# Layer 0's node loop: loads queued behind the x tiles, degree sums on TensorE, reciprocal by Ln and Exp

## The chip, the cores and the metric

The kernel runs on one core of a Trainium2 chip. The metric is the device time of one execution in microseconds; the time of a kernel is the median of several runs. Profiles come from one profiled execution each. TensorE is written PE, VectorE DVE, ScalarE ACT, GpSimd POOL and SyncE SP, as in the profile.

## What is computed

The reference is a network of four layers, each `x = x + layer(relu(layernorm(x)))`, over x of 8 batches × 2048 nodes × 64 features with a 0/1 adjacency of 2048 × 2048. Only layer 0, attention over the hyperedges of an incidence matrix H (2048 × 64), is touched:

```python
h = x @ W                                   # x: layernorm and relu done
alpha = softmax(where(H.T > 0, leaky_relu(h @ a_node), NEG))   # over nodes
agg = einsum('ben,bnf->bef', alpha, h)
beta = sigmoid((h @ a_gn)[:, None, :] + (agg @ a_ge)[:, :, None])
all_he = elu(beta[..., None] * h[:, None] + (1 - beta[..., None]) * agg[:, :, None])
deg = maximum(adj.sum(-1), 1.0)[:, None]
industry = einsum('nm,bmf->bnf', adj / deg, x @ W_ind)
coefs1 = softmax(where(H > 0, attn_scores(elu(agg)), NEG))
g = einsum('bne,benf->bnf', coefs1, all_he)
coefs2 = softmax(attn_scores(stack([industry, g])))
out = einsum("bnk,bnkf->bnf", coefs2, stack([industry, g]))
```

Layers 1 (graph attention), 2 (three message steps) and 3 (node-wise weights) follow and use the same adjacency.

## The kernel before

**Tiling.** P is 128 partitions, and the 2048 nodes are NT = 16 tiles of 128. A node tile of x has all 8 batches beside each other, 128 × 512. The 8 batches × 64 features are also NP = 4 blocks of 128 in the transposed form hn[p]. The adjacency is read in NCW = 4 chunks of CW = 512 columns, each as eight pairs of row tiles `at` (512 KB a load, through POOL's DMA queue, six buffers, `rows_of` at L893). `acc[p]` are the four PSUM sums of one chunk.

**Layer 0's loop** (L976 to L990) norms the 16 x tiles, maps them by W_ind and at once multiplies them into chunk 0 of the adjacency. It is software-pipelined over 21 iterations j, and each step has a lag in tiles: `sums` (DVE reduce and scale), `centred` (POOL subtraction, xc), `squares` (ACT), `sums2` (DVE reduce), `scales` (ACT Ln, Exp), `scaled` (DVE, xc times the scale), `turns` (PE, four transposes into tpx), `turned` (ACT, four copies into hn), `maps` (PE, four matmuls into py), `halves` (ACT copy to Y[0], DVE rest to Y[1]), and `spread` (PE, eight matmuls into acc). `degrees` (L963) adds the adjacency pairs on POOL into ds. x tiles are loaded through SP by `load`, three tiles ahead, five buffers. M (H, two loads) and MT (H transposed, `HT`) are loaded through SP ahead of the loop, at L972 to L974.

**Order.** Inside the loop the steps are issued through `InOrder` wrappers V, A and G (L622), which keep program order on DVE, ACT and POOL; with `kit.strict` PE's matmuls keep it too. Instructions issued otherwise are placed by a scheduler, which may move them ahead in their engine's queue, as far as their data and buffers allow. In the kernel before, SP's loads are of this second kind, and so are `weights` (L810, the small weights of the layer), `marks` (L1172, `is_gt 0` on M and MT), `listing` (hyperedge ranks) and what follows.

**Behind the loop** `out_of(0)` (L1023) empties chunk 0, and `industry(c)` (L1004) does chunks 1 to 3, 128 matmuls each. Between its matmuls it takes small jobs off a list `units`, three for each adjacency pair: for each node tile `members` (the W matmuls ph, split in hi and lo parts, which go to hi_dram and lo_dram through SP, and sums for agg), the listing, the weights of layers 1 and 2 with their loads, and hyperedge tables. `out_of` copies acc to ev, sums ds over partitions by two matmuls with ones (deg), takes twice the maximum with 1 (rdeg), its reciprocal on DVE, multiplies the four ev by it and stores them to ind_dram. Then the phase over node tiles and slots begins with `nodes(0)` (ACT tmp, POOL sT), `ranks` (PE px), `edges` (DVE oT) and the pm matmuls, and copies xT to x1_dram in DRAM for layer 1.

Of the kernel before, what the change touches and what calls it, by code (L numbers as in the profile page):

```python
# [16 lines left out]
P = 128  # L17
B, N, F = 8, 2048, 64
E = 64
NP = B // 2  # L20
# [614 lines left out]
class Kit:  # L635


    def __init__(self, tc, t, pool):
        nc = self.nc = tc.nc
        self.tc, self.t, self.strict = tc, t, False  # L640
# [24 lines left out]
    def column(self, pool, src, name):  # L665
        c = pool.tile([P, 1], FP, name=name)
        for b2 in range(2):
            self.nc.sync.dma_start(out=c[half(b2), :], in_=src)
        return c
# [5 lines left out]
    def block_diag_in(self, w, src):  # L675
        self.nc.vector.memset(w, 0.0)
        for b2 in range(2):
            self.nc.sync.dma_start(out=w[half(b2), half(b2)], in_=src)
        return w

    def layer1_weights(self, pool, ps):

        nc, t = self.nc, self.t
# [3 lines left out]
        nc.vector.memset(a4, 0.0)  # L687
        for b2 in range(2):
            nc.sync.dma_start(out=a4[half(b2), b2 : b2 + 1], in_=t["L1_gnn_a"][F : 2 * F, :])
            nc.sync.dma_start(out=a4[half(b2), 2 + b2 : 3 + b2], in_=t["L1_gnn_a"][0:F, :])  # L690
# [5 lines left out]
    def layer2_weights(self, pool, ps):  # L696

        nc, t, mm = self.nc, self.t, self.nc.tensor.matmul
# [3 lines left out]
        W2n = self.block_diag(pool, t["L2_gnn_W2"], "W2n", "wd")  # L702
        for dst, src in ((self.b1, "b1"), (self.b2c, "b2"), (self.ivc, "intervention_value")):
            for b2 in range(2):
                nc.sync.dma_start(out=dst[half(b2), :], in_=t[f"L2_gnn_{src}"])

        for dst, w in ((self.Wvc, self.W1v), (self.Wec, self.W1e)):
# [51 lines left out]
def layer0(kit, hn, x1_dram, open_early, late_tile, between):  # L759
# [9 lines left out]
    w0 = ctx.enter_context(tc.tile_pool(name="v0", bufs=1, reuse_waits="tile"))  # L769
    dram = ctx.enter_context(tc.tile_pool(name="h_dram", bufs=1, space=DRAM))  # L770
# [29 lines left out]
    with ExitStack() as sA:  # L800
# [9 lines left out]
        def weights(pool, ps):  # L810

            W = kit.block_diag(pool, t["L0_gnn_W"], "W0f", "wd")
            WT = kit.block_diag(pool, t["L0_gnn_WT"], "W0Tf", "wt")
            a2 = pool.tile([P, 4], FP, name="a2")
            nc.vector.memset(a2, 0.0)
            for b2 in range(2):
                nc.sync.dma_start(out=a2[half(b2), b2 : b2 + 1], in_=t["L0_gnn_a_node"])
                nc.sync.dma_start(out=a2[half(b2), 2 + b2 : 3 + b2], in_=t["L0_gnn_a_gn"])
            nc.sync.dma_start(out=a_ge, in_=t["L0_gnn_a_ge"].rearrange("f o -> o f").to_broadcast([P, F]))
            nc.sync.dma_start(out=fcb, in_=t["L0_gnn_fcb"])  # L820
            nc.sync.dma_start(out=av, in_=t["L0_gnn_av"])
            for b2 in range(2):
                nc.sync.dma_start(out=fcW[half(b2), :], in_=t["L0_gnn_fcW"])
            nc.vector.tensor_scalar(Av, ones, av, None, op0=OP.mult)
            nc.vector.tensor_copy(Wx[:, 0:P], W)
            pw = ps.tile([P, 4], FP, tag="ph", name="pw", bufs=2)
            mm(pw, WT, a2, start=True, stop=True)
            nc.vector.tensor_copy(Wx[:, P : P + 4], pw)

        def listing(ps):  # L830
# [4 lines left out]
            def slots():  # L835
                tmp = lst.tile([P, SLOTS], mybir.dt.int32, tag="hhi", name="iota_i", bufs=3)
                nc.gpsimd.iota(tmp, pattern=[[1, SLOTS]], base=0, channel_multiplier=0)
                nc.vector.tensor_copy(slot, tmp)
# [3 lines left out]
                nc.vector.tensor_copy(tri, ti)  # L842
# [47 lines left out]
        aps = sA.enter_context(tc.tile_pool(name="a_ps", bufs=1, space=PSUM, reuse_waits="tile"))  # L890
        accs = lambda: [aps.tile([P, CW], FP, tag=f"acc{p}", name=f"acc{p}") for p in range(NP)]
# [9 lines left out]
        with ExitStack() as s1:  # L901
            sb = s1.enter_context(tc.tile_pool(name="nf_sb", bufs=2, reuse_waits="tile"))
            ps = s1.enter_context(tc.tile_pool(name="nf_ps", bufs=2, space=PSUM, reuse_waits="tile"))
            V, A, G = InOrder(tc, nc.vector), InOrder(tc, nc.scalar), InOrder(tc, nc.gpsimd)
            acc, ds = accs(), dsp.tile([P, 2, CW], FR, tag="ds", name="ds")
# [4 lines left out]
            def load(i):  # L910
                xs[i] = sb.tile([P, B * F], FP, tag="x", name="x", bufs=5)
                nc.sync.dma_start(out=xs[i], in_=t["xN"][i * P : (i + 1) * P, :])
# [25 lines left out]
            def turns(i):  # L938
                tp[i] = ps.tile([P, NP, P], FP, tag="tp", name="tpx")
# [22 lines left out]

            def degrees(g):  # L963
                if g:
                    G.tensor_tensor(ds, (at[0] if g == 1 else ds).bitcast(FP), at[g].bitcast(FP), op=OP.add)
# [6 lines left out]
            for h in range(2):  # L972
                nc.sync.dma_start(out=M[:, :, h, :], in_=t["L0_gnn_H"].rearrange("(t p) e -> p t e", p=P))
            nc.sync.dma_start(out=MT, in_=t["HT"])  # L974
            kit.strict = True
            for j in range(NT + 5):  # L976
                on = lambda k: 0 <= j - k < NT
                if 0 < j and j + 3 < NT:
                    load(j + 3)
                for lag, step in (  # L980
                    (0, sums), (0, centred), (1, squares), (1, sums2), (2, turns), (3, maps),
                    (4, halves), (1, scales), (1, scaled), (2, turned), (5, spread),
# [4 lines left out]
                if m > 0 and m % 2:  # L987
                    degrees(m // 2)
                    if 1 <= m // 2 and m // 2 + 5 < NT // 2:
                        at[m // 2 + 5] = rows_of(0, m // 2 + 5)  # L990
            kit.strict = False

        with ExitStack() as s1:
            sb = s1.enter_context(tc.tile_pool(name="e_sb", bufs=2, reuse_waits="tile"))
            ps = s1.enter_context(tc.tile_pool(name="e_ps", bufs=1, space=PSUM, reuse_waits="tile"))
            ones_r = sb.tile([P, P], FR, name="ones_r", bufs=1)
            for h in range(2):
                nc.vector.tensor_copy(ones_r[:, half(h)], ones)
# [5 lines left out]
            def industry(c):  # L1004

# [1184 lines left out]
```

## Time and profile before

| | us |
|---|---|
| median of 3 runs (lowest, highest) | 2018.38 (2016.62, 2019.0) |
| profiled execution, its time | 2020.19 |
| profiled execution, its span | 2018.3 |
| PE busy in the span | 1926.3 (95%) |
| DVE, ACT, POOL busy | 1232.7 (61%), 437.2 (22%), 343.2 (17%) |
| chunk 0's loop: first and last acc matmul | 40.1, 95.5 |
| end of chunk 3's acc matmuls | 257.0 |

The span is what the profiler saw of the program; 1.9 us of the execution lie around it. Busy times of engines overlap. Row L630 and row L723 are lines of helpers that issue on behalf of many steps, so groups are told apart by the names of their tiles. "A<-B" reads: written A, read B.

### The profile page before, as it was taken

To read this page: it belongs to the slowest core of one execution; us is meant where nothing else is said; L and a number is where in the kernel's file an instruction comes from. 1 tells how busy PE (TensorE), PEld (TensorE's weight loads), DVE (VectorE), ACT (ScalarE), POOL (GpSimd) and SP (SyncE) were. 2 spreads that over 40 slices of the span, in tenths; PEclk is the share of its full clock that TensorE was granted. 3 is DMA by queue.
4 is the path that set the end of the run, shared out by engine and by line. 5 is a ranking of instruction groups with operands and counts; after the bars stand their busy time and mean duration, and the time that the engine had idled before them with its cause. 6 is when DMAs were issued, how large, how long until landed. Compare 5 with 4: busy or idle time off the path is not lost.

```text
span 2018.3 us, 23591 instructions
## 1 busy us (share of the span) xinstructions
PE 1926.3 (95%) x9092; PEld 1148.0 (57%) x9092; DVE 1232.7 (61%) x1940; ACT 437.2 (22%) x907; POOL 343.2 (17%) x446
## 2 busy tenths in 40 slices
PE   3899999987999999999999999999999999999997
PEld 3777767632322222226776467775477755577653
DVE  5867489966899999893234752326632356523365
ACT  3422145557211111111130011210111200112100
POOL 3511057621000000000001210002200012101022
PEclk9999889999999999999999999999999999999999
DMA  7467256156212222214110012201022100122000
GB/s 185 147 183 206 85 174 200 47 151 146 67 48 58 48 58 53 53 43 102 53 48 18 22 38 65 58 13 31 23 64 61 32 21 20 44 68 57 4 20 12
DMA packets 85786, 142.41 MB, mean 71 GB/s; under 512 B 33232, under 2 KB 33488, under 8 KB 82992
## 3 DMA queue, kind: packets, MB, share of 16 engines
q1 hardware_dynamic: 65200, 83.86, 14.3%
q0 software_dynamic: 20464, 56.96, 11.3%
q8 instruction: 73, 1.20, 0.2%
q14 instruction: 49, 0.40, 0.1%
HBM read 106.84 MB, written 37.09 MB: 71 GB/s over the span
## 4 chain that ended last, share of the span: by engine, by line
PE 59%; issue 20%; DVE 8%; DMA 7%; ACT 3%; POOL 2%; SPq 1%; POOLq 0%; DVEq 0%; ACTq 0%
PE acc L723 23%; PE u L723 13%; PE o L723 3%; PE pd L723 3%; PE pgs L723 2%; PE acc L1013 2%; PE py L723 2%; DMA den<-d_dram 2%; DMA at<-in_adjT 2%; PE dn L723 1%; PE pm L723 1%; DVE xc L630 1%; PE mean L723 1%; PE var L723 1%; DVE pt L1663 1%
## 5 line engine op out<-in xcount | busy, mean ns | idle before, releaser
L723 PE MATMUL acc<-aT,parts 128*128 128x512 f32 x1664 | 448.3, 415 | 0.0
L723 PEld LDWEIGHTS acc<-aT,parts 128*128 128x128 f32 x1664 | 306.5, 188 | 102.2 <-issue 39.8
L2065 DVE TENSOR_TENSOR pr<-u,embf 128x512 f32<-128x512 f32 x256 | 170.6, 687 | 170.8 <-PE u L723 163.8
L1663 DVE SCALAR_TENSOR_TENSOR pt<-R,wd,aT 128x1024 f32<-128x1024 f32 x192 | 235.9, 1277 | 9.5 <-DMA R<-r_dram 2.7
L723 PE MATMUL u<-W3f,y 64*128 64x512 f32 x1024 | 241.2, 589 | 0.0
L723 PE MATMUL o<-pt,hS 128*64 128x512 f32 x1024 | 237.3, 599 | 0.8 <-DVE pt L1663 0.6
L723 PEld LDWEIGHTS u<-W3f,y 64*128 64x128 f32 x1024 | 99.8, 187 | 120.0 <-issue 120.0
L723 PEld LDWEIGHTS o<-pt,hS 128*64 128x64 f32 x1024 | 68.3, 136 | 160.1 <-issue 148.6
L723 PE MATMUL u<-W3f,v 64*128 64x512 f32 x512 | 135.8, 607 | 0.0
L2077 POOL TENSOR_TENSOR fold<-fold 128x256 f32<-128x256 f32 x64 | 47.7, 746 | 505.8 <-DVE fold L2076 505.8
L723 PE MATMUL dn<-pt,vd 128*32 128x512 f32 x1024 | 123.1, 598 | 0.0
L1882 DVE TENSOR_TENSOR yb<-py,cb_f 128x512 f32<-128x512 f32 x32 | 22.1, 691 | 161.3 <-PE py L723 161.3
L1013 PE MATMUL acc<-at,Y 128*128 128x512 f32 x384 | 109.1, 425 | 1.1 <-DVE ev L1026 1.1
L723 PE MATMUL acc<-aTl,parts 128*128 128x512 f32 x384 | 96.5, 393 | 0.0
L1972 POOL TENSOR_TENSOR bq<-bq,xp 128x512 f32<-128x512 f32 x16 | 20.6, 1287 | 433.5 <-ACT xp L1955 433.5
L2069 DVE TENSOR_TENSOR pr<-pr 128x512 f32<-128x512 f32 x128 | 88.1, 688 | 2.2
L1663 DVE SCALAR_TENSOR_TENSOR pt<-R,wd,aTl 128x1024 f32<-128x1024 f32 x64 | 79.8, 1281 | 12.4 <-PE dn L723 8.2
L723 PEld LDWEIGHTS u<-W3f,v 64*128 64x128 f32 x512 | 50.5, 186 | 55.9 <-issue 34.1
L1013 PEld LDWEIGHTS acc<-at,Y 128*128 128x128 f32 x384 | 71.6, 196 | 18.2 <-issue 3.5
L723 PEld LDWEIGHTS acc<-aTl,parts 128*128 128x128 f32 x384 | 72.1, 188 | 16.9
L630 POOL TENSOR_TENSOR mix<-ex,wt 128x512 f32<-128x512 f32 x64 | 67.8, 1061 | 34.6 <-DVE ex L630 27.6
L723 PEld LDWEIGHTS dn<-pt,vd 128*32 128x32 f32 x1024 | 26.9, 108 | 80.9 <-issue 76.3
(343 smaller groups left out, 2758.5 us busy)
## 6 DMA issues: line engine op xcount, KB each, us to landing
at<-in_adjT POOLq DMA_DIRECT2D x32, 512.0 KB, 5.1
raw<-in_adjT SPq DMA_DIRECT2D x64, 256.0 KB, 3.4
aT<-in_adjT POOLq DMA_DIRECT2D x12, 1024.0 KB, 5.2
xp<-xd SPq DMA_DIRECT2D x45, 256.0 KB, 3.4
R<-r_dram SPq DMA_DIRECT2D x14, 512.0 KB, 3.7
hi_dram<-hi SPq DMA_DIRECT2D x16, 264.0 KB, 3.0
lo_dram<-lo SPq DMA_DIRECT2D x16, 264.0 KB, 3.3
hlo<-lo_dram POOLq DMA_DIRECT2D x16, 264.0 KB, 3.2
```

The lines of the kernel that those rows point to most:

```text
L630: self.tc.keep_in_program_order(getattr(self.engine, name)(*args, **kw))
L723: one = self.nc.tensor.matmul(*args, **kw)
L1013: mm(acc[p], Y[h][:, m, p, :], at[:, k, :], start=m + h == 0, stop=m == NT - 1 and h == 1)
L1663: nc.vector.scalar_tensor_tensor(pt, R[b2], wd[:, m, b2 : b2 + 1], aT[m][:, s].bitcast(FP), op0=OP.max, op1=OP.mult)
L1882: nc.vector.tensor_tensor(yb, py, bias[:, None, :].to_broadcast([P, 4, P]), op=OP.add)
L1972: nc.gpsimd.tensor_add(bq, bq, xp)
L2065: nc.vector.tensor_tensor(a, u[h], emb[:, i, 8 * w : 8 * w + 8, None].to_broadcast([P, 8, F]), op=OP.mult)
L2069: nc.vector.tensor_add(pr[h], pr[h], a)
L2077: nc.gpsimd.tensor_add(fold[:, :, 0:2, :], fold[:, :, 0:2, :], fold[:, :, 2:4, :])
```

## The change

- V, A, G and a new S for SP are made at the top of layer0. x tiles are loaded through S. Loads of M and MT move behind the loop, behind x tile 15 in S's order, the marks behind it on V.
- The first small weights are loaded through S at j == 6 in the loop, the others behind MT. The loads of layers 1 and 2 (8 and 14 DMAs) become units of their own, through S; the copies of xT to x1_dram go through S too.
- Chunk 0's degree sums: a matmul of each adjacency row tile with a matrix of ones into a PSUM tile deg0, in `spread`; `degrees` on POOL and chunk 0's two deg matmuls go. The transposes' PSUM tile has one buffer for two.
- The loop's steps are put in another order: `spread` stands ahead of `turns` and `turned`, `maps` and `halves` ahead of `scales`. The next adjacency pair is asked for directly behind the `spread` that ends the use of its buffer.
- `out_of` returns its last steps as a list: Ln and Exp on ACT for the reciprocal (with the factor 2 in Ln's scale), and four multiplies with their stores; they are taken one by one in the slots of the next chunk, chunk 3's directly behind it.
- `industry` takes two units ahead of its matmuls; listing steps are put into 12 slots for 8; Av is made in table_3.

```diff
+    V, A, G, S = (InOrder(tc, e) for e in (nc.vector, nc.scalar, nc.gpsimd, nc.sync))
...
+        small = sA.enter_context(tc.tile_pool(name="small_w", bufs=1, reuse_waits="tile"))
+        kit.sync = S
+        a2 = small.tile([P, 4], FP, name="a2")
+        nc.vector.memset(a2, 0.0)
+
+        def loads():
+
+            W = kit.block_diag(small, t["L0_gnn_W"], "W0f", "wd")
+            WT = kit.block_diag(small, t["L0_gnn_WT"], "W0Tf", "wt")
             for b2 in range(2):
-                nc.sync.dma_start(out=a2[half(b2), b2 : b2 + 1], in_=t["L0_gnn_a_node"])
-                nc.sync.dma_start(out=a2[half(b2), 2 + b2 : 3 + b2], in_=t["L0_gnn_a_gn"])
-            nc.sync.dma_start(out=a_ge, in_=t["L0_gnn_a_ge"].rearrange("f o -> o f").to_broadcast([P, F]))
-            nc.sync.dma_start(out=fcb, in_=t["L0_gnn_fcb"])
-            nc.sync.dma_start(out=av, in_=t["L0_gnn_av"])
+                S.dma_start(out=a2[half(b2), b2 : b2 + 1], in_=t["L0_gnn_a_node"])
+                S.dma_start(out=a2[half(b2), 2 + b2 : 3 + b2], in_=t["L0_gnn_a_gn"])
+            return W, WT
...
+        def weights(ps, W, WT):
+
+            S.dma_start(out=a_ge, in_=t["L0_gnn_a_ge"].rearrange("f o -> o f").to_broadcast([P, F]))
+            S.dma_start(out=fcb, in_=t["L0_gnn_fcb"])
+            S.dma_start(out=av, in_=t["L0_gnn_av"])
             for b2 in range(2):
-                nc.sync.dma_start(out=fcW[half(b2), :], in_=t["L0_gnn_fcW"])
-            nc.vector.tensor_scalar(Av, ones, av, None, op0=OP.mult)
-            nc.vector.tensor_copy(Wx[:, 0:P], W)
+                S.dma_start(out=fcW[half(b2), :], in_=t["L0_gnn_fcW"])
+            V.tensor_copy(Wx[:, 0:P], W)
...
+        ones_r = ypool.tile([P, P], FR, name="ones_r")
+        for h in range(2):
+            nc.vector.tensor_copy(ones_r[:, half(h)], ones)
+        degs = dsp.tile([P, 2, CW], FR, tag="ds", name="ds")[:, 0, :].bitcast(FP)
...
-            V, A, G = InOrder(tc, nc.vector), InOrder(tc, nc.scalar), InOrder(tc, nc.gpsimd)
-            acc, ds = accs(), dsp.tile([P, 2, CW], FR, tag="ds", name="ds")
+            acc = accs()
+            deg0 = ps.tile([P, CW], FP, tag="deg0", name="deg0", bufs=1)
...
-                nc.sync.dma_start(out=xs[i], in_=t["xN"][i * P : (i + 1) * P, :])
+                S.dma_start(out=xs[i], in_=t["xN"][i * P : (i + 1) * P, :])
...
-                tp[i] = ps.tile([P, NP, P], FP, tag="tp", name="tpx")
+                tp[i] = ps.tile([P, NP, P], FP, tag="tp", name="tpx", bufs=1)
...
-            def degrees(g):
-                if g:
-                    G.tensor_tensor(ds, (at[0] if g == 1 else ds).bitcast(FP), at[g].bitcast(FP), op=OP.add)
+                kit.mm(deg0, ones_r, at[m // 2][:, m % 2, :], start=m == 0, stop=m == NT - 1)
 
             kit.use_ln_exp()
             for i in range(4):
                 load(i)
             for g in range(6):
                 at[g] = rows_of(0, g)
-            for h in range(2):
-                nc.sync.dma_start(out=M[:, :, h, :], in_=t["L0_gnn_H"].rearrange("(t p) e -> p t e", p=P))
-            nc.sync.dma_start(out=MT, in_=t["HT"])
             kit.strict = True
             for j in range(NT + 5):
                 on = lambda k: 0 <= j - k < NT
                 if 0 < j and j + 3 < NT:
                     load(j + 3)
+                if j == 6:
+                    first = loads()
                 for lag, step in (
-                    (0, sums), (0, centred), (1, squares), (1, sums2), (2, turns), (3, maps),
-                    (4, halves), (1, scales), (1, scaled), (2, turned), (5, spread),
+                    (0, sums), (0, centred), (1, squares), (1, sums2), (3, maps), (4, halves),
+                    (1, scales), (1, scaled), (5, spread), (2, turns), (2, turned),
                 ):
                     if on(lag):
                         step(j - lag)
                 m = j - 5
-                if m > 0 and m % 2:
-                    degrees(m // 2)
-                    if 1 <= m // 2 and m // 2 + 5 < NT // 2:
-                        at[m // 2 + 5] = rows_of(0, m // 2 + 5)
+                if m > 0 and m % 2 and m // 2 + 6 < NT // 2:
+                    at[m // 2 + 6] = rows_of(0, m // 2 + 6)
             kit.strict = False
+            V.tensor_copy(degs, deg0)
+            for h in range(2):
+                S.dma_start(out=M[:, :, h, :], in_=t["L0_gnn_H"].rearrange("(t p) e -> p t e", p=P))
+            S.dma_start(out=MT, in_=t["HT"])
...
-            def industry(c):
-
+            def industry(c, own):
+
+                for _ in range(2):
+                    units.pop(0)()
...
+                            if own:
+                                own.pop(0)()
 
                     if g > 0:
                         nc.vector.tensor_tensor(ds, (was if g == 1 else ds).bitcast(FP), at.bitcast(FP), op=OP.add)
                     was = at
-                out_of(c, acc, ds)
+                return out_of(c, acc, ds)
...
+                deg = ds
+                if c:
+                    deg = ps.tile([P, CW], FP, tag="ph", name="deg", bufs=2)
+                    for k in range(2):
+                        mm(deg, ones_r, ds[:, k, :], start=k == 0, stop=k == 1)
                 rdeg = sb.tile([P, CW], FP, tag="rdeg", name="rdeg", bufs=1)
+                nc.vector.tensor_scalar(rdeg, deg, 1.0, None, op0=OP.max)
                 nc.vector.tensor_reduce(bad[:, 3 + c : 4 + c], deg, AX.X, OP.min)
                 nc.vector.tensor_scalar(bad[:, 3 + c : 4 + c], bad[:, 3 + c : 4 + c], 0.5, None, op0=OP.is_lt)
 
-                nc.vector.tensor_scalar(rdeg, deg, 1.0, 2.0, op0=OP.max, op1=OP.mult)
-                nc.vector.reciprocal(rdeg, rdeg)
-                for p in range(NP):
+                def inverse():
+                    nc.scalar.activation(rdeg, rdeg, AF.Ln, scale=2.0)
+                    nc.scalar.activation(rdeg, rdeg, AF.Exp, scale=-1.0)
+
+                def shares(p):
                     nc.vector.tensor_mul(ev[p], ev[p], rdeg)
                     nc.sync.dma_start(out=ind_dram[p, :, cols(c)], in_=ev[p])
+
+                return [inverse] + [lambda p=p: shares(p) for p in range(NP)]
...
-                nc.vector.tensor_scalar(Mf, Mf, 0.0, None, op0=OP.is_gt)
-                nc.vector.tensor_scalar(MT, MT, 0.0, None, op0=OP.is_gt)
-
-            small = s1.enter_context(tc.tile_pool(name="small_w", bufs=1, reuse_waits="tile"))
-            weights(small, ps)
+                V.tensor_scalar(Mf, Mf, 0.0, None, op0=OP.is_gt)
+                V.tensor_scalar(MT, MT, 0.0, None, op0=OP.is_gt)
+
             marks()
+            weights(ps, *first)
+            kit.sync = nc.sync
...
+            def loads_2():
+                kit.sync = S
+                held[2] = kit.layer2_loads(small)
+                kit.sync = nc.sync
...
+            rest[3:3] = [loads_2]
+            rest[1:1] = [loads_1]
+            rest += [lambda: kit.layer1_weights(ps, *held[1]), lambda: kit.layer2_weights(small, ps, held[2])]
             for i in range(NT):
                 begin_, part_, end_ = members(i)
                 units += [begin_, part_] + ([last] if last else [])
-                if i % 2 and rest:
+                if i % 4 and rest:
...
-            out_of(0, acc, ds)
+            own = out_of(0, acc, degs)
             for c in range(1, NCW):
-                industry(c)
-            while units:
-                units.pop(0)()
+                own = industry(c, own)
+            for unit in own + units:
+                unit()
...
-            nc.sync.dma_start(out=x1_dram[p], in_=t["xT"][p])
+            S.dma_start(out=x1_dram[p], in_=t["xT"][p])
```

## The prediction

> **What bounds the kernel now.** I first read the page's slices: they show where TensorE, which fills 95% of the span, is not busy.
>
> ```profile
> span 2018.3 us, 23591 instructions
> ...
> PE   3899999987999999999999999999999999999997
> ...
> PEclk9999889999999999999999999999999999999999
> ```
>
> A slice is 50 us. The first is at 3 tenths, and slices 2, 3 and 8 are not full; everything from the tenth on is TensorE's. Layer 0's loop lies in the first two slices, so what it can give back is idle TensorE time there. The second view is the chain of waits of the first 100 us (start, length, what).
>
> ```profile
> 4.72 8.18 SPq L973
> 12.94 12.15 DMA MT<-in_HT
> 25.11 1.23 DVE MT L1175
> 26.40 2.17 issue
> 28.57 0.67 DVE st L630
> ...
> 49.13 2.89 DVE xc L630
> ...
> 56.85 2.83 DVE xc L630
> ```
>
> The start is not held by x or the adjacency but by H: SP issues M's second load for 8.18 us, MT lands 12.15 us after its issue began, and only then does VectorE go on to the second sums of tile 0 (28.57). Why VectorE waits there is in the third view, the timeline (start, busy, engine, work, in brackets the idle time before it):
>
> ```profile
> 22.53 1.23 DVE L1174 TENSOR_SCALAR M<-M 128x2048 f32<-128x2048 f32 x1 [16.40 <-DMA M<-in_L_gnn_H]
> 25.11 1.22 DVE L1175 TENSOR_SCALAR MT<-MT 64x2048 f32<-64x2048 f32 x1 [1.35 <-DMA MT<-in_HT]
> 26.37 2.28 DVE L883 TENSOR_REDUCE bad<-MT 64x1 f32<-64x2048 f32 x1
> 28.57 0.67 DVE L630 TENSOR_REDUCE st<-x 128x8 f32<-128x512 f32 x1
> ...
> 49.08 2.40 POOL L630 TENSOR_TENSOR ds<-at 128x1024 fp32r<-128x1024 f32 x1
> 49.11 2.91 DVE L630 SCALAR_TENSOR_TENSOR xc<-xc,st 128x512 f32<-128x512 f32 x1
> ```
>
> The marks of M and MT belong behind the loop in the source; the scheduler has put them and a check of MT ahead of tile 0's second sums, in an engine that works in order. The last two lines are the loop's other loss: an xc scaling that takes 0.69 us at 46.35 takes 2.91 beside a degree sum of POOL. The last view is busy time by stretch (stretch, length, then TensorE, weight loads, VectorE, ScalarE, POOL, clock, DMA share, GB/s):
>
> ```profile
> 0.00:30.00 30.00, 0.00 (x0) 0.00 (x0) 10.08 (x28) 2.61 (x5) 7.91 (x16) 1.00 0.85 205
> 30.00:92.00 62.00, 52.93 (x306) 45.03 (x307) 57.56 (x89) 34.25 (x125) 35.58 (x27) 0.97 0.50 153
> ```
>
> TensorE does nothing for 30 us, then idles 9 of 62; the loop's last acc matmul ends at 95.5.
>
> **What the Trainium skill says.** "SBUF — State Buffer", *Who interferes with whom*: a VectorE instruction with two SBUF inputs contends with a GpSimd instruction that reads SBUF, and who issues first blocks the other. The trace agrees: 2.91 against 0.69 us. "TensorE: Matmul & The Clock Gate", *Part 1: The HAM clock gate*: after an idle window of about 3.4 us the array falls to half rate until it has been busy as long. The trace agrees in kind, though shorter gaps are enough here: after a gap of 2.63 us at 112.74 the clock is half from 115.4 to 118.8, and after one of 2.55 us inside the loop from 81.3 to 84.7. "ScalarE: Activation LUTs", *What ACT_TABLE_LOAD costs*: 1283 ns, plus a drain of some 1380 for a switch; the trace has 1.28 us for the load at 0.73.
>
> **The change, part by part.**
>
> *Start.* M's two loads and MT's go behind x tile 15 on SP, the marks go behind the loop on VectorE, x tile 4 is no longer queued behind 13.9 us of issuing (8.88 + 5.00). ScalarE's square of tile 0 begins at 7.24 and takes 0.63, so its second sums can run at 7.9 instead of 28.57: **−20.6 us**. What is late next: x tiles 2 and 3, issued at 2.9, land some 6.5 us later (about 9.5), one to two us behind. From 28.57 to the first acc matmul (40.13) were 11.6 us; behind a start at 7.9, with spread now ahead of the fourth tile's transposes, I take the first acc at 17.3, a gain of 22.8, of which the part beyond 20.6 belongs to the reordering and is repaid in the loop's length below.
>
> *The loop from first to last acc.* Before: 40.1 to 95.5, 55.4 us. After: each of 16 tiles has 8 acc matmuls (8 × 0.2325 = 1.86) and one more for the degree sum (0.23); 13 tiles have four maps (0.89) and four transposes (0.44) inside the stretch: 33.5 + 11.6 + 5.7 = 50.8. The nine-matmul spread adds 16 × 0.23 = 3.7. It takes away what POOL did: 7 degree sums × 2.4 us, and with them the idle TensorE time they caused through xc: 0.32 + 3 × 1.06 + 2.55 = 6.05 us, and half of the 3.4 us at half clock, 1.7. The new order puts maps(i) directly behind turns(i), with ScalarE's four copies between (before, maps of an earlier tile and a whole spread stood there), and the transposes' PSUM tile is single. Its cost isn't in the trace of before: from below nothing is excluded (0), from above the four copies as the row hn<-tpx gives them, 4 × 0.275 = 1.1; the first map needs only the first copy, so I take 0.4 × 13 = 5.2. Loop: 56.0, end at 17.3 + 56 = 73.3 against 95.5. **Start and loop together −22** (−16 to −26).
>
> POOL's queue: its remaining adjacency loads now wait for the spread of the tile pair that frees a buffer, and the next xc subtraction is queued behind each; that xc is needed three tiles (about 10 us) later, against 1.04 + 0.65 + 0.68 + 0.5 + 0.69 = 3.6 us of chain, so it is costed at nothing. SP's queue: eight small weight loads (0.55 each, 4.4 us) stand between x tiles 9 and 10; x is loaded three tiles, about 10 us, ahead: nothing, covered by that.
>
> *From the loop's end (95.5) to the end of chunk 3 (257.9), 162.4 us.* Idle TensorE gaps there are 2.63, 0.95, 0.39, 2.55, 0.71 and 2.91 (10.1 us), and half-clock stretches behind them cost some 6.8. Removed: three reciprocals of 3.3 us on VectorE inside chunks (99.21, 153.28 and an end), in exchange for Ln and Exp (about 0.6 each) on ScalarE, which is a fifth busy; the four multiplies go one by one into later slots instead of in a row; two deg matmuls of chunk 0. Added: the marks (1.23 + 1.22) on VectorE ahead of W0x's copies, with the check of MT further back; the first ph matmul, which needs W0x, may come 2.5 us later, but 16 acc matmuls (3.7 us) lie ahead of it: nothing. 22 small loads for layers 1 and 2 (22 × 0.55 = 12 us of SP) now stand between hi and lo stores, whose buffers VectorE's memset of hi and lo waits for: a wait of 2.63 us of that kind is at 112.74 already. Bounds: −14 if gaps and cold stretches nearly all go, +6 if two or three new waits of 2.6 us come. I take **−6**.
>
> *The end of chunk 3.* Its scalings have no next chunk to be spread over. ScalarE gets table load, Ln, table load, Exp ahead of tmp; VectorE gets four multiplies ahead of oT. Before:
>
> ```profile
> 257.57 0.72 ACT L630 ACTIVATE tmp<-slot,mid 128x512 f32<-128x512 f32 x1
> ...
> 259.22 3.35 DVE L1035 RECIPROCAL rdeg<-rdeg 128x512 f32<-128x512 f32 x1
> ...
> 262.49 0.63 DVE L630 TENSOR_TENSOR oT<-px,slot 128x512 fp32r<-128x512 f32 x1
> ```
>
> After: rdeg's max ends at 259.2, Ln 259.8, second table load 261.1, Exp 261.7, four multiplies of 0.62 to 264.2, oT behind them against 262.49; **+2.5** (1 to 5, with the drain that the skill states).
>
> *The copies of xT to x1 in DRAM* leave 47 to 57 us (7.9 us each to land) for SP's rows around chunk 3's stores, beside aT's first loads: **+0.5** (0 to 4).
>
> Sum: −22 − 6 + 2.5 + 0.5 = **−25**. The profiled execution is 2020.2 us (span 2018.3 and 1.9 around it), 1.8 above the median of the runs, 2018.4. So the execution becomes 1995.2, the median about **1993.4**.
>
> **Rivals.**
> 1. *The loop gains, and M is late instead.* M and MT are issued behind x tile 15, whose buffer comes free with tile 10, at about 40 us. With 13.9 us of issuing and 12.2 of landing they are there by 66 to 70, with the loop ending at 73. For it: M took 16 us to land under load. Against: DMA's share falls behind the first 30 us (0.85 to 0.50). If the marks wait 8 to 10 us, W0x behind them waits, and the gain is about 15: 2003.
> 2. *More gain.* The gaps and half-clock stretches behind the loop go nearly all (−14 for −6), and the junction's table loads are hidden: −34, 1984. Against: most of these gaps end on hs, lo and ev, not on the reciprocal.
> 3. *Slower: maps behind turned.* ScalarE works in order, and turned(i) stands behind Ln of another tile, which waits for VectorE's second sums, which wait for ScalarE's square. If that chain (0.65 + 0.68 + 0.5) and the copies (0.76) are not under the spread, each tile waits about 2.8 us rather than 0.4: 13 × 2.4 = 31 us, against a gain of 25: 2024. The turning point is a wait of 0.4 + 25/13 = 2.3 us per tile. Against: spread and maps are 3 us of TensorE work, longer than the chain.
> 4. *It doesn't do what it says*: the scheduler puts the marks ahead again. The order of the built kernel has them behind the loop, so this has next to no chance: 2018.
>
> **How the numbers follow.** The forecast has 0.58, rival 1 0.13, rival 2 0.20, rival 3 0.07, rival 4 0.02. The first three are faster by over 0.2% (4 us, about what a measurement of this kernel can tell from no change): 0.91 faster, 0.02 same, 0.07 slower. The likeliest case gives 1993.4. Adding the ends of its terms would be wider than they go together; rival 2 below (to 1981) and rival 1 above (to 2007) set the range.
>
> **What would show it.** In the profile after: first sums2 near 8 us and first acc at 17 to 19; no POOL ds in chunk 0's loop and no xc of 2.9 us; the loop's last acc near 73, with gaps of 0.4 us ending on ScalarE's copies; M's marks directly behind it, with no idle time from DMA; the first TensorE idle time behind 73 below 10 us in all up to chunk 3's end, which falls near 230; px and oT 2 to 3 us later against that end. Wrong it would be by: maps waiting over 1 us, marks waiting for DMA M, hi stores late behind the small loads, or x tiles waiting behind weight loads.

## The result and the profile after

The kernel after takes 1998.2 us (median of 4 runs, 1996.0 to 2000.5) against 2017.5 (4 runs, 2011.7 to 2019.0): a ratio of 0.991, 95% interval 0.989 to 0.993, or 13 to 23 us less. The profiled executions, which the sum was made on, are 2020.2 and 1996.0 us (spans 2018.3 and 1994.1): 24.2 less, where 25 were forecast; the medians are 19.3 apart. The profiled execution of before is slower than all four of its runs, that of after is the fastest of its four.

The page's slices, after:

```profile
span 1994.1 us, 23643 instructions
...
PE   7999899978999999999999999999999999999997
...
PEclk9999799989999999999999999999999999999998
```

The first slice is at 7 tenths rather than 3: TensorE starts 20 us earlier. The fifth (200 to 250 us) still holds the junction behind chunk 3, and a half-clock stretch.

The chain of waits of the first 80 us (start, length, what; the helpers' lines L723 and L729 of before are L733 and L739 here):

```profile
4.66 1.48 POOL at L916 x2
6.14 1.08 POOL xc L630
...
7.25 0.64 ACT x L630
7.91 0.70 DVE st L630
...
18.44 1.16 PE py L733 x8
19.59 1.84 PE acc L733 x8
21.67 0.45 PE tpx L739 x4
22.47 1.16 PE py L733 x8
```

The second sums of tile 0 run at 7.91; M and MT are out of the chain. It now begins in POOL's queue: tile 0's subtraction stands behind the issuing of six adjacency loads, up to 6.14 us, though its sums on VectorE were done at 4.36. By these two figures some 1.8 us may lie there, an estimate that no run tested. From 18 us on the chain is TensorE's own work, with a hole of 0.35 us a tile between tpx and py. The timeline shows what stands in that hole, and where M went (start, busy, engine, work, in brackets the idle time before it):

```profile
42.67 1.16 PE L733 MATMUL py<-W_indf,hn 128*128 128x128 f32 x8 [0.37 <-ACT hn L630]
...
44.39 0.33 SPq L630 DMA_DIRECT2D x<-in_xN  x1
44.77 3.00 SPq L630 DMA_DIRECT2D M<-in_L_gnn_H  x2
...
45.75 0.60 PE L739 MATMUL tpx<-ident_f,xc 128*128 128x128 f32 x4
46.38 0.79 ACT L630 ACTIVATE hn<-tpx 128x128 f32<-128x128 f32 x4 [1.45 <-PE tpx L739]
46.71 1.16 PE L733 MATMUL py<-W_indf,hn 128*128 128x128 f32 x8 [0.37 <-ACT hn L630]
47.63 2.09 PE L733 MATMUL acc<-at,Y 128*128 128x512 f32 x8
47.81 2.09 SPq L630 DMA_DIRECT2D MT<-in_HT  x1
...
78.95 1.40 DVE L630 TENSOR_SCALAR M<-M 128x2048 f32<-128x2048 f32 x1
80.27 1.20 DVE L630 TENSOR_SCALAR MT<-MT 64x2048 f32<-64x2048 f32 x1
```

A tile takes 4.04 us (46.71 − 42.67). M and MT are asked for at 44.8 to 49.9 us, and the marks at 78.95 wait for no DMA.

Stage by stage, from the two traces (last row: from the second px of the slot phase to the span's end):

| us | before | after | difference |
|---|---|---|---|
| first acc matmul at | 40.1 | 19.4 | −20.8 |
| from there to the loop's last copy to ev | 55.4 | 58.8 | +3.3 |
| from there to chunk 3's last acc | 161.5 | 151.8 | −9.7 |
| from there to the second px | 11.1 | 14.8 | +3.7 |
| rest | 1750.2 | 1749.4 | −0.8 |

In the thirteen profiled executions of this study the rest is between 1745 and 1757 us, on code that no kernel changed. So a difference of a few us between kernels is read from the stages, and the runs' medians only decide where it is larger.

### The profile page after: what moved, and what is told of

Same layout as the page of the kernel before. It is cut to its first block, busy times and chain, and to the rows that moved or that the text cites. A ratio compares the mean times of both kernels' runs of the same rounds, so it can differ in the third digit from the quotient of the medians.

```text
span 1994.1 us, 23643 instructions
## 1 busy us (share of the span) xinstructions
PE 1925.6 (97%) x9106; PEld 1145.1 (57%) x9106; DVE 1206.6 (61%) x1937; ACT 445.9 (22%) x917; POOL 327.7 (16%) x439
## 3 DMA queue, kind: packets, MB, share of 16 engines
q0 software_dynamic: 20464, 56.96, 11.6%
## 4 chain that ended last, share of the span: by engine, by line
PE 68%; issue 16%; DVE 5%; DMA 4%; ACT 3%; POOL 3%; SPq 0%; POOLq 0%; DVEq 0%; ACTq 0%
PE acc L733 25%; PE u L733 13%; PE o L733 7%; PE dn L733 3%; PE py L733 3%; PE pd L733 3%; PE pgs L733 3%; PE acc L1031 2%; PE var L733 1%; PE mean L733 1%; DMA iv<-ind_dram 1%; DMA den<-d_dram 1%; PE pm L733 1%; PE pv L733 1%; DVE pt L1705 1%
## 5 line engine op out<-in xcount | busy, mean ns | idle before, releaser
L733 PE MATMUL acc<-aT,parts 128*128 128x512 f32 x1664 | 448.2, 415 | 0.0
L733 PEld LDWEIGHTS acc<-aT,parts 128*128 128x128 f32 x1664 | 306.5, 188 | 102.2 <-issue 39.8
L733 PE MATMUL u<-W3f,y 64*128 64x512 f32 x1024 | 241.2, 589 | 0.0
L733 PE MATMUL o<-pt,hS 128*64 128x512 f32 x1024 | 237.4, 599 | 0.8 <-DVE pt L1705 0.6
L733 PEld LDWEIGHTS u<-W3f,y 64*128 64x128 f32 x1024 | 99.8, 187 | 120.0 <-issue 120.0
L733 PEld LDWEIGHTS o<-pt,hS 128*64 128x64 f32 x1024 | 68.3, 136 | 160.1 <-issue 148.8
L733 PE MATMUL u<-W3f,v 64*128 64x512 f32 x512 | 135.8, 607 | 0.0
L733 PE MATMUL dn<-pt,vd 128*32 128x512 f32 x1024 | 123.1, 598 | 0.0
L733 PE MATMUL acc<-aTl,parts 128*128 128x512 f32 x384 | 96.5, 393 | 0.0
L733 PEld LDWEIGHTS u<-W3f,v 64*128 64x128 f32 x512 | 50.5, 186 | 55.9 <-issue 33.9
L733 PEld LDWEIGHTS acc<-aTl,parts 128*128 128x128 f32 x384 | 72.1, 188 | 17.0
L733 PEld LDWEIGHTS dn<-pt,vd 128*32 128x32 f32 x1024 | 26.9, 108 | 80.9 <-issue 76.3
```

What stands on the lines that cost most here:

```text
L733: one = self.nc.tensor.matmul(*args, **kw)
```

## The experiments

Ratios are to the kernel before, which ran beside each group on the same chip. The stages are of one profile each:

| kernel | median us | ratio, 95% interval | first acc | loop end | chunk 3's last acc | second px |
|---|---|---|---|---|---|---|
| after | 1998.2 | 0.991 (0.989–0.993) | 19.4 | 78.1 | 229.9 | 244.7 |
| e1_move_alone | 2003.0 | 0.994 (0.992–0.997) | 31.8 | 87.7 | 244.1 | 254.8 |
| e2_loads_ahead | 2009.1 | 0.997 (0.996–0.998) | 29.0 | 89.3 | 241.0 | 255.8 |
| e3_sums_on_pool | 2002.9 | 0.995 (0.993–0.996) | 19.5 | 85.3 | 236.3 | 251.1 |
| e11_sums_held | 1997.1 | 0.991 (0.988–0.994) | 19.1 | 75.5 | 227.0 | 241.8 |
| e4_turns_ahead | 1988.7 | 0.987 (0.984–0.991) | 19.3 | 69.3 | 222.9 | 237.7 |
| e5_reciprocal | 1993.7 | 0.990 (0.988–0.992) | 19.4 | 78.1 | 229.7 | 241.1 |
| e6_no_spreading | 2003.1 | 0.995 (0.993–0.997) | 18.9 | 77.6 | 231.5 | 246.4 |
| e10_old_slots | 1999.1 | 0.992 (0.991–0.994) | 19.4 | 78.2 | 225.8 | 250.0 |
| e7_last_on_dve | 1995.2 | 0.990 (0.988–0.992) | 18.9 | 77.7 | 228.1 | 239.5 |
| e8_one_table | 1992.9 | 0.989 (0.985–0.994) | 19.1 | 77.8 | 234.8 | 248.3 |
| e9_both | 1983.3 | 0.985 (0.983–0.986) | 19.3 | 69.3 | 217.1 | 228.4 |

**The start: the move alone, and the loads alone.**

```diff
 # e1_move_alone, from before: M, MT behind the loop, x in order, marks in order
+            V, A, G, S = (InOrder(tc, e) for e in (nc.vector, nc.scalar, nc.gpsimd, nc.sync))
-                nc.sync.dma_start(out=xs[i], in_=t["xN"][i * P : (i + 1) * P, :])
+                S.dma_start(out=xs[i], in_=t["xN"][i * P : (i + 1) * P, :])
...
-                nc.vector.tensor_scalar(Mf, Mf, 0.0, None, op0=OP.is_gt)
+                V.tensor_scalar(Mf, Mf, 0.0, None, op0=OP.is_gt)
```

> The kernel before with one part of the change: loads of M and MT and the marks behind the loop, x tiles loaded in program order. The other small loads stay where the scheduler puts them. Theory (it takes marks and small loads together to hold the start): second sums of tile 0 no longer wait for M (28.6 us), but in VectorE's order they now stand behind the copy of W1f into W1x, and W1f is the twentieth load on SP, some 16 x 0.55 = 9 us behind the fifth x tile's issue, so second sums near 15 us, x tile 5 behind 28 small loads at some 20 us; first acc near 27, loop as before: gain about 12 us, 2005. Rival (M and the marks alone held the start): second sums at 7.9, gain 20, 1997. Rival (the start is bound by x and the adjacency landing under load): no gain over 3 us.

Second sums of tile 0 came at 20.24, first acc at 31.8: 8.4 us earlier than before, of the 20.8 that the whole change won. The timeline of this run says what took M's place:

```profile
14.24 0.23 DVE L825 COPY W0x<-W0f 128x128 f32<-128x128 f32 x1 [8.82 <-DMA W0f<-in_L_gnn_W]
...
18.94 0.25 DVE L824 TENSOR_SCALAR Avf<-ones_f,avf 128x64 f32<-128x64 f32 x1 [4.22 <-DMA avf<-in_L_gnn_av]
...
19.84 0.23 DVE L691 COPY W1x<-W1f 128x128 f32<-128x128 f32 x1 [0.64 <-DMA W1f<-in_L_gnn_W]
...
20.24 0.63 DVE L630 TENSOR_REDUCE st<-x 128x8 f32<-128x512 f32 x1
```

Three operations on small weights (W0x, Avf, W1x), each behind its own DMA, stand ahead of the sums in VectorE's order. The expectation named W1x alone and put the sums at 15; the mechanism is as expected and 5 us larger. So the gain at the start needs the marks and the small weights moved together.

```diff
 # e2_loads_ahead, from after: M and MT are loaded through S ahead of the loop
                 at[g] = rows_of(0, g)
+            for h in range(2):
+                S.dma_start(out=M[:, :, h, :], in_=t["L0_gnn_H"].rearrange("(t p) e -> p t e", p=P))
+            S.dma_start(out=MT, in_=t["HT"])
```

> The kernel after with M's and MT's loads ahead of the loop on SP again; the marks stay behind the loop on VectorE. Theory (both places matter): 13.9 us of issuing stand between x tiles 3 and 4, so x tile 4 lands near 21 rather than 14 us and the loop from there on is 6 to 8 us later: 2005. Rival (only the marks' place in VectorE's order held the start; SP's queue is covered by the four tiles already loaded): 0 to +1 us, 1999.

The loop ended 11.2 us later than in after, and SP's queue is the reason:

```profile
5.22 7.98 SPq L630 DMA_DIRECT2D M<-in_L_gnn_H  x1
...
13.24 4.94 SPq L630 DMA_DIRECT2D MT<-in_HT  x1
...
18.23 8.56 SPq L630 DMA_DIRECT2D x<-in_xN  x5
24.95 0.69 DVE L630 TENSOR_REDUCE st<-x 128x8 f32<-128x512 f32 x1 [9.46 <-DMA x<-in_xN]
```

x tile 4 isn't issued before 18.23, and VectorE waits 9.46 us for it. That is more than the 6 to 8 us expected, which had tile 4 landed near 21 us. Both places count: VectorE's order and SP's queue.

**The loop: the order of turns, and the degree sums.**

```diff
 # e4_turns_ahead, from after
-                    (1, scales), (1, scaled), (5, spread), (2, turns), (2, turned),
+                    (1, scales), (1, scaled), (2, turns), (5, spread), (2, turned),
```

> The kernel after with turns put ahead of spread in the loop's order (PE: maps, turns, spread), so that ScalarE's copies lie under the spread. Theory (the loop is longer than reckoned because maps directly behind turned wait 0.36 us and run at the copies' pace, 1.16 rather than 0.89 us): 13 x 0.63 = 8 us off the loop, a pace of 3.4 us for 4.04, 1990. Rival (VectorE or ScalarE in order are next, near 3.4 to 4 us a tile): the wait moves to xc and 0 to 3 us are gained, 1996.

The loop ended at 69.3, 8.8 us earlier than after, and the hole is gone. Its timeline:

```profile
41.64 0.39 PE L733 MATMUL deg<-at,ones_r 128*128 128x512 f32 x1
41.87 1.05 PE L733 MATMUL py<-W_indf,hn 128*128 128x128 f32 x8
42.76 0.60 PE L739 MATMUL tpx<-ident_f,xc 128*128 128x128 f32 x4
43.12 2.08 PE L733 MATMUL acc<-at,Y 128*128 128x512 f32 x8
...
45.27 1.05 PE L733 MATMUL py<-W_indf,hn 128*128 128x128 f32 x8
```

A tile takes 3.40 us rather than 4.04 (45.27 − 41.87). So maps directly behind turned cost 0.64 us a tile. Where it lies: from the start of the transposes to the next matmul are 0.36 us here (42.76 to 43.12), 0.96 in after (45.75 to 46.71). The copies can't begin before the transposes have come out (0.60 rather than the 0.36 for which they hold TensorE), and the first takes another 0.36. The expectation had put part of it down to slower maps; these take 0.92 us to the next matmul in after and 0.89 here.

```diff
 # e3_sums_on_pool, from after: POOL adds the adjacency pairs, as before the change
-                kit.mm(deg0, ones_r, at[m // 2][:, m % 2, :], start=m == 0, stop=m == NT - 1)
+            def degrees(g):
+                if g:
+                    G.tensor_tensor(ds, (at[0] if g == 1 else ds).bitcast(FP), at[g].bitcast(FP), op=OP.add)
...
 # e11_sums_held, from e3
-                        nc.vector.tensor_tensor(ds, (was if g == 1 else ds)...
+                        (V if c == 1 else nc.vector).tensor_tensor(ds, (was if g == 1 else ds)...
```

> The kernel after with chunk 0's degree sums on POOL again and without the matmuls with ones in the loop. Theory: PE loses 16 x 0.23 = 3.7 us of work, but seven xc scalings take 2.9 us again rather than 0.7, and VectorE's load of 2.9 us a tile rises to 4.0 on the mean, above PE's 3.8; loop about 2 us longer, whole 0 to +6: 2000. Rival (the new order hides the lock fully): -3.7 us, 1994.5. Rival (each lock reaches PE whole): +15 - 4 = +11, 2009.

The loop ended 7.2 us later, so it looked as if the degree sums on TensorE were worth that. The timeline spoke against it:

```profile
56.55 1.23 DVE L1041 TENSOR_TENSOR ds<-at 128x1024 fp32r<-128x1024 f32 x1 [3.38 <-DMA at<-in_adjT]
...
59.24 1.01 PE L733 MATMUL py<-W_indf,hn 128*128 128x128 f32 x3 [2.90 <-ACT hn L630]
```

L1041 is chunk 1's first degree sum. In this kernel the scheduler had taken it into the loop, and VectorE stood 3.38 us waiting for an adjacency load of chunk 1, with x's tiles behind it. So e3 mixes two things, and e11 takes the second away.

> Chunk 0's degree sums on POOL as in e3_sums_on_pool, and chunk 1's first sums kept behind the loop in VectorE's order; in e3 they stood in the loop, waiting 3.38 us for their adjacency load, and both long waits of PE (2.90 and 3.96 us) lay beside them. Theory (with the new order POOL's lock is hidden; what e3 lost were the moved sums): a pace of 3.81 us a tile, last ev copy of the loop at 75 rather than 78, -3 against after: 1995. Rival (the lock reaches PE by itself, once the pairs come in a row): waits over 1 us on xc or hn remain and the loop ends at 80 or later: 2000 to 2003.

Now the loop ends at 75.5, 2.6 us earlier than in after. Its longest xc scaling is 2.80 us and the median of the twelve from 21.3 us on is 1.14, so POOL's lock is there, yet from 18.2 us on every idle gap of TensorE over 0.3 us in the loop is 0.36 or 0.37, the hole behind turned. With spread between scaled and turns, the lock no longer reaches TensorE. In this order the degree matmuls are paid in full and bring nothing: from the first to the last acc matmul the loop takes 55.3 us against 58.7, about the 16 × 0.23 us of their work. The copies to ev then come late by 1 us for another reason:

```profile
72.61 2.27 DVE L900 TENSOR_REDUCE bad<-MT 64x1 f32<-64x2048 f32 x1
...
74.88 1.27 DVE L1048 COPY ev<-acc 128x512 f32<-128x512 f32 x2
```

The check of MT, which after has at 110 us, stands ahead of them on VectorE. The run's median (1997.1) can't tell e11 from after; the stage can, for the loop takes the same time within 0.1 us in e5, e6, e7, e8 and e10, where it is that of after. Whether the degree matmuls pay where turns stand ahead of spread, as in e4 and e9, was not tried.

**Chunks 1 to 3: the reciprocal, the spreading, the slots.**

```diff
 # e5_reciprocal, from after
-                    nc.scalar.activation(rdeg, rdeg, AF.Ln, scale=2.0)
-                    nc.scalar.activation(rdeg, rdeg, AF.Exp, scale=-1.0)
+                    nc.vector.tensor_scalar(rdeg, rdeg, 2.0, None, op0=OP.mult)
+                    nc.vector.reciprocal(rdeg, rdeg)
...
 # e6_no_spreading, from after
-                return [inverse] + [lambda p=p: shares(p) for p in range(NP)]
+                inverse()
+                for p in range(NP):
+                    shares(p)
+                return []
...
 # e10_old_slots, from after
-                for _ in range(2):
-                    units.pop(0)()
...
-                if i % 4 and rest:
+                if i % 2 and rest:
```

> The kernel after with the reciprocal on VectorE again (a doubling and the 3.3 us reciprocal) in place of Ln and Exp; the multiplies stay spread over the slots, and chunk 3's stay directly behind it. Theory (half of the 9.7 us won between the loop's end and chunk 3's end comes from VectorE's freed time): chunks 1 to 3 take 152 to 157 us rather than 151.8, and the junction behind chunk 3 is 1 to 4 us shorter, as no table is loaded: 1998 in all, 0 to +2 against after. Rival (the reciprocal was what made TensorE wait there): +8, 2006. Rival (VectorE has room, the reciprocal cost nothing): the junction's gain stands alone, -3, 1995.

From the loop's end to chunk 3's last acc it took 151.6 us against 151.8, with 5.4 us of idle TensorE against 5.8: the third way, no cost of the reciprocal is seen there. One profile can't show a small one: e2, e4, e7, e8 and e9 have after's code in this stretch and take 151.7, 153.6, 150.5, 156.9 and 147.8 us for it, with 5.3 to 7.7 us of idle TensorE. Behind chunk 3 it was 3.5 us shorter (11.35 against 14.83).

> The kernel after with Ln, Exp and the four multiplies with their stores issued in a row in out_of rather than one by one in the next chunk's slots. Theory (what lets the next chunk start is that VectorE isn't held): the multiplies are 4 x 0.65 us in a row, chunks 1 to 3 take 2 to 4 us longer than 151.8: 2001. Rival (spreading is worth nothing, since the scheduler puts the multiplies where there is room anyway): 0, 1998.

153.9 against 151.8 us; idle TensorE rose from 5.8 to 8.8, with a gap of 2.87 at 145.84 and one of 2.25 at 94.29. The runs too are slower, 0.995 against 0.991, with intervals that hardly overlap. So spreading very likely brings something, but its size is open: 2.1 us in a stretch that scatters by more, some 8 us by the ratios. And what lies ahead of the two gaps is not a VectorE held by the multiplies, as expected, but a wait for stores:

```profile
83.94 2.12 SPq L1063 DMA_DIRECT2D ind_dram<-ev  x4
86.61 0.32 SPq L1106 DMA_DIRECT2D hi_dram<-hi  x1
...
93.11 0.07 DVE L1082 MEMSET hi<- 128x8 f32 x1 [3.62 <-DMA hi_dram<-hi]
...
96.55 0.69 PE L1089 MATMUL ph<-W0x,hn 128*128 128x132 f32 x4 [2.25 <-DVE es L1097]
```

VectorE waits 3.62 us for a hi store issued behind the four stores of ev; in the second case ScalarE waits 3.50 us, up to 144.97, for a hi store that was again issued behind four of ev.

> The kernel after with the small jobs placed as before: no two units ahead of a chunk's matmuls, listing steps in every second node tile. Theory (of the 9.7 us won in chunks 1 to 3, no more than 2.1 come from spreading and none from the reciprocal; the place of the jobs gives part of the rest): chunks 1 to 3 take 153 to 156 us rather than 151.8, the whole 2000 to 2002. Rival (the place of jobs is worth nothing; the rest comes with the marks and loads having left the start): 151 to 152.5 us, 1998.

Both ways were wrong: the last acc came 4.1 us earlier (225.8), but work left over from the list, the pn and pb matmuls that run among the accs in after, now stood behind it, and the second px came at 250.0, 5.3 us later than in after. Idle TensorE up to the last acc was 8.4 us against 5.8, so the stalls didn't get shorter either; the last acc comes early because 40 fewer matmuls lie ahead of it. What counts is what is left at the end. The runs (0.992 against 0.991) don't tell the two kernels apart.

**The junction behind chunk 3.** Timeline of after:

```profile
230.59 1.28 ACT L1058 ACT_TABLE_LOAD   x1
...
231.89 0.63 ACT L1058 ACTIVATE rdeg<-rdeg 128x512 f32<-128x512 f32 x1
232.53 1.28 ACT L1059 ACT_TABLE_LOAD   x1
233.83 0.63 ACT L1059 ACTIVATE rdeg<-rdeg 128x512 f32<-128x512 f32 x1
234.36 0.71 ACT L630 ACTIVATE tmp<-slot,mid 128x512 f32<-128x512 f32 x1
234.49 2.91 DVE L1062 TENSOR_TENSOR ev<-ev,rdeg 128x512 f32<-128x512 f32 x4 [2.60 <-ACT rdeg L1059]
235.18 2.56 POOL L630 TENSOR_SCALAR sT<-tmp,width 128x512 fp32r<-128x512 f32 x1 [45.84 <-ACT tmp L630]
...
237.79 0.80 PE L733 MATMUL px<-sT,Q 128*128 128x512 f32 x1 [7.43 <-POOL sT L630]
```

The first px comes 7.9 us behind the last acc, against 3.0 before. tmp stands behind both table loads, Ln and Exp, and sT takes 2.56 us rather than 1.56, beside VectorE's multiplies.

```diff
 # e7_last_on_dve, from after: in inverse()
+                    if c == NCW - 1:
+                        nc.vector.tensor_scalar(rdeg, rdeg, 2.0, None, op0=OP.mult)
+                        nc.vector.reciprocal(rdeg, rdeg)
+                        return
...
 # e8_one_table, from after: in inverse()
+                    if c == NCW - 1:
+                        kit.use_ln_exp()
```

> The kernel after with chunk 3's reciprocal alone on VectorE (a doubling and a reciprocal, no tables). Theory (the junction is 3.7 us longer than before through two table loads of 1.28, Ln and Exp, and one lock of POOL's sT beside VectorE's multiplies): from chunk 3's last acc to the second px 11 to 12 us rather than 14.8, and so -3 to -3.7 in all: 1995. Rival (the chain goes over multiplies and oT whatever makes the reciprocal): VectorE's 0.7 + 3.3 + 2.9 stand ahead of oT and the junction stays at 14 to 15.

From the last acc to the second px 11.35 us for 14.83, −3.5. tmp runs at once and sT is through before most of the reciprocal; oT then waits for it, so the second px gains less than the first (4.8 us):

```profile
228.66 0.72 ACT L630 ACTIVATE tmp<-slot,mid 128x512 f32<-128x512 f32 x1
...
229.50 1.62 POOL L630 TENSOR_SCALAR sT<-tmp,width 128x512 fp32r<-128x512 f32 x1 [40.70 <-ACT tmp L630]
...
230.57 3.34 DVE L1060 RECIPROCAL rdeg<-rdeg 128x512 f32<-128x512 f32 x1
231.17 0.51 PE L733 MATMUL px<-sT,Q 128*128 128x512 f32 x1 [2.60 <-POOL sT L630]
```

> The kernel after with the joint Ln and Exp table loaded by name ahead of chunk 3's Ln: one load rather than two between ev and tmp, and one again behind the first tmp. Theory: the second load (1.28 us) leaves the path to tmp: first px 6.6 us behind the last acc rather than 7.9, -1.3 in all: 1997. Rival (the load that now stands behind the first tmp delays nodes(1), and the second px comes no earlier): 0.

13.55 us for 14.83: −1.28, one table load, to the hundredth. Its last acc came 4.9 us later than in after, with a half-clock stretch from 221 to 232, so the median decides nothing here.

**Both repairs together.**

> The kernel after with both repairs: turns ahead of spread, and chunk 3's reciprocal on VectorE. Theory (the two lie in different stretches and add): last ev copy of the loop at 69 to 70 us, from chunk 3's last acc to the second px 11.3 us as with the reciprocal alone, so 8.8 and 3.5 us less than after: 1986. Rival (what the loop gains returns as waits of VectorE in chunk 1, where 1.8 us more came with turns ahead alone): 1990.

1983.3 us, ratio 0.985 (0.983 to 0.986): 31 us below the kernel before by the ratio, beyond the interval of after. The loop ends at 69.3 and the junction takes 11.35, each as alone. Chunks 1 to 3 took 147.8 us with a mean clock of 0.99, so the rival's lost waits did not come; about 4 of the 16.8 us between the two profiles' spans come from that stretch, which the edits don't touch.

## Why the prediction was right

The side and the path were right, and the median lies inside the range. That the size agrees so well, 24.2 us less for 25 on the profiled executions, is in part luck: start and loop gave 4.6 us less than forecast, chunks 1 to 3 gave 3.7 us more, and by the medians the change is worth 19.3 us.

- **The start** was forecast to the second sums at 7.9; they came at 7.91. The first acc came at 19.4 for 17.3, 11.4 us behind these sums, as before the change (11.6). The 2.2 us taken off for the new order didn't come: the maps of the first two tiles take 2.08 and 2.07 us, those of the third 1.16, and in before only the first tile's were as slow (1.92 at 34.20, 1.05 at 36.94). The move alone (e1) shows that the term needed more than its text said: not only the marks but three small operations had to leave VectorE's order.
- **The loop** was to take 56.0 us and took 58.8. The step that was mis-sized is "the first map needs only the first copy, so I take 0.4": it measured 0.64 a tile (e4). The copy was counted, the 0.24 us that the transposes need to come out was not. e4, without the hole, takes 50.0 us where the work was reckoned at 50.8; so the hole costs 8.8 us for the 5.2 put down. Start and loop together gave −17.4 for −22, with the stated range −16 to −26.
- **The degree sums** were taken as a good exchange: 3.7 us of TensorE for 6 us of idle time and a half-clock stretch. e11 refutes that as a sum of parts: with the new order of steps the idle time behind POOL's lock goes by itself, and the matmuls cost their 3.4 us.
- **POOL's and SP's queues** were costed at nothing. In the loop of after no idle TensorE time is ended by x or an adjacency load, which agrees.
- **Loop's end to chunk 3's end**: −9.7 for −6 (to the last acc; the 257.9 of the working is the end of the deg matmuls). The working put the gain down to the removed reciprocals and the spreading. e5 shows no cost of the first, and e6 shows the second in part. What changed can be read from the busy time by stretch (stretch, length, TensorE, weight loads, VectorE, ScalarE, POOL, clock, DMA share, GB/s), of before and then of after:

```profile
95.50:257.00 161.50, 151.27 (x718) 119.55 (x717) 94.98 (x283) 33.89 (x116) 16.84 (x25) 0.93 0.51 154
```

```profile
78.00:230.00 152.00, 146.20 (x718) 114.68 (x716) 92.84 (x294) 37.17 (x123) 16.82 (x25) 0.97 0.56 171
```

The same 718 matmul records. Idle TensorE fell by 4.4 us (10.23 to 5.80), and the time lost to the clock from about 0.07 × 161.5 = 11 to 0.03 × 152 = 5 us. Where it was lost, the gaps and the clock by stretch show. These are the three longest gaps of before, then the longest of after:

```profile
115.37 1.17 PE L1059 MATMUL ph<-W0x,hn 128*128 128x132 f32 x4 [2.63 <-DVE lo L1052]
165.35 0.69 PE L1059 MATMUL ph<-W0x,hn 128*128 128x132 f32 x4 [2.55 <-DVE hs L1070]
218.45 0.56 PE L693 MATMUL pw<-a,W1Tf 128*128 128x4 f32 x2 [2.91 <-issue]
```

```profile
161.90 0.69 PE L1086 MATMUL ph<-W0x,hn 128*128 128x132 f32 x4 [1.63 <-DVE es L1095]
```

In before, half-clock stretches of 3.4, 3.4 and 6.8 us begin at 115.4, 166.6 and 217.8, all within 1.3 us of the end of such a gap, and cost about half their length, 6.8 us, as the prediction reckoned. In after there is none of this kind. The other loss, 4.2 us in before (half clock from 248.5 on) and 5.1 in after (215.6 to 225.8), follows no gap over 0.11 us in the 24 us ahead. In the six profiles that have after's code here (after, e2, e4, e7, e8, e9), half clock behind gaps costs 0 to 3.4 us and the other kind 1.7 to 5.1. So the forecast's mechanism, fewer gaps and less half clock behind them, fits the record, with more of it than the −6 taken.

The Trainium skill's "TensorE: Matmul & The Clock Gate", *Part 1: The HAM clock gate*, names idle windows as the cause; the three gaps agree, though shorter than its 3.4 us, and the stretches without a gap don't. Nor is every gap followed by half clock: not those of 2.55 us at 71.36 in e1 and 2.25 at 94.29 in e6. Which edit removed the gaps is not shown: e6 and e10 bring gaps of over 2 us back, but so does e8 (2.51 at 160.75) with after's code, and e1, which has neither spreading nor new slots, already takes 156.4 us.
- **The junction** was +2.5 and measured +3.7. The two table loads were named, ahead of tmp too, but the path was worked over oT alone (264.2 for 262.49, which gives 1.7 and not 2.5): tmp, sT and px stand behind both loads at once, and sT is then held by the multiplies (2.56 for 1.56). The table load itself is 1.28 us in the trace, as "ScalarE: Activation LUTs", *What ACT_TABLE_LOAD costs*, has it; its further 1.38 us of drain isn't seen: Ln ends at 232.52, the load begins at 232.53, and Exp at 233.83.
- **The copies of xT** show no cost: the rest of the program is 0.8 us shorter in these two profiles, within its scatter. They weren't tried alone.
- **The step to the median** was the weakest. It took 1.8 us off because before's profiled run stood that far above its median; after's stood 2.2 below. That, not the work, makes most of the 1998.2 for 1993.4.
- **The rivals.** M and MT were not late: 5.1 us of issuing from 44.8 for the 13.9 of the start. Maps waited 0.36 us, far from the 2.3 at which slower begins. The scheduler did not move the marks back. One sign of being wrong did show, once: VectorE waits 3.66 us for a hi store at 158.34, but no small load stands ahead of that store, and TensorE lost 1.6 us there.

## What to carry to other kernels

Where a scheduler may move work ahead, it can put work in front of a loop whose load is still under way, and an engine in order then waits for it, as VectorE did here: look for the first instruction of each engine whose wait is long, and move all its fellows, since the next one takes its place. When two edits cure the same stall, take each away alone: here the order of steps hid POOL's lock, and the matmuls meant to avoid it were pure cost in that order. Where work that is spread over a next stage has no next stage at the end, what stands behind it there sets its price.

## What the runs showed of the hardware that was not expected

- SP's time to issue the M loads depends on when: 7.98 us for the second one at the start (e2), 3.00 for both in the middle of the loop (after), and the median time to land fell from 16.0 us (before) to 6.8.
- TensorE's first matmuls run at about half pace: the maps at 12.16 and 15.46 take 2.08 and 2.07 us for eight, those at 18.44 take 1.16. The clock of 1.00 in the stretch of the first 30 us doesn't speak against it: the trace has no clock record ahead of 17.60 us, and time without a record is counted as full.
- Half clock came not only behind gaps of TensorE (2.55 to 2.91 us in before) but also with no gap over 0.11 us in the 24 us ahead (215.6 to 225.8 in after).
- POOL's sT with one SBUF tensor in beside VectorE's multiply with two took 2.56 us rather than 1.56: the loser is whoever comes second, here POOL, as "SBUF — State Buffer", *Who interferes with whom*, says.
